# The grouped convolution of a four-layer network on one core: from three-row stacks on four column tiles to 32x32 products on sixteen tiles

## The chip, the cores and the metric

The kernel runs on one core of one Trainium2 chip. The time is the device time of one execution in microseconds (us), as a median over runs. The engines have short names throughout: PE is TensorE's matmul, PEld its weight load, DVE is VectorE, ACT is ScalarE, POOL is GpSimd, SP is SyncE, which here only issues DMAs.

## The reference

The input is a batch of 8 images of 128 channels and 56x56 pixels, all float32. Four layers follow one another, each a residual over a group norm of 32 groups of 4 channels:

```python
def _L2_conv_ref(x, w3, w1, b, p):
    O, I = (w3.shape[0], w3.shape[1])
    i = jnp.arange(O)[:, None]
    j = jnp.arange(I)[None, :]
    m3 = (j - i) % p == 0
    w3m = w3 * m3[:, :, None, None].astype(w3.dtype)
    out = jax.lax.conv_general_dilated(x, w3m, window_strides=(1, 1), padding=((1, 1), (1, 1)), dimension_numbers=('NCHW', 'OIHW', 'NCHW'))
    w1m = w1 * (~m3).astype(w1.dtype)
    out = out + jnp.einsum('oi,bihw->bohw', w1m, x)
    out = out + b.sum(axis=1)[None, :, None, None]
    return out
...
    x = x + _L0_conv_ref(_gn(x), ...)
    x = x + _L1_conv_ref(_gn(x), ...)
    x = x + _L2_conv_ref(_gn(x), L2_conv_w3, L2_conv_w1, L2_conv_b, 4)
    x = x + _L3_conv_ref(_gn(x), ...)
```

Layer 0 is window attention with a depthwise 3x3 convolution. Layer 1 is a recurrence over the 3136 pixels of an image, with 512 hidden values, h = tanh(g + W h). Layer 2, whose code is shown, is a 3x3 convolution in which an output channel sees only the input channels of its own class (index modulo 4), and a 1x1 convolution in which it sees only the channels of the other three classes. Layer 3 is two full 3x3 convolutions with batch norms and a residual.

## The kernel before

The residual stream `X` stays in SBUF, 128 channels on 128 partitions, 8 images of 3136 pixels in the free dimension. The channels are sorted by class, so each class is one quarter of 32 partitions (`CL` = 32). An image has seven blocks of eight rows (`NBLK` = 7, `WS` = 8, 448 pixels), which is one PSUM bank of float32.

**Layer 1** works on 17 pieces of every image at once (`NCH`), two time steps per turn of its loop: per step `step` (L1078) multiplies the gates on PE, DVE adds the input's share (L1098) and ACT takes the tanh (L1100). In the first 186 steps the input's share is computed in the same turn (`shrunk`, L1015: tanh on ACT at L1026, then the subtraction on DVE at L1027; `products`, `gathered`); in the last 56 it is read back from DRAM (`recall`). As pixels become final, `stats` (L983) takes batch norm statistics (`bn_stats`) of the final stretch of image 0, so that layer 2 finds them ready: 8 instructions in all.

**Layer 2** is in `convolutions`. Each image is normalised into a padded copy `pads[b % 2]` of 58x58. `spread` (L1304) makes `g3` from it: for each class three copies of its 32 channels, shifted by 0, 1 and 2 columns, stacked on 96 partitions, so that one product covers the three taps of a row. Of the 12 copies of a chunk of rows, 3 lie on the right partitions and are made by ACT (L1315); 9 cross partitions and are DMAs, issued from the queues of SP and POOL (L1317). An image is spread in three chunks (the first image in five). Per block, `within` (L1321) runs 12 products 96x32: three rows of taps by four classes, each class on its own 32 columns of the array and its own 32 partitions of the bank. `between` (L1332) adds the masked 1x1 as one 128x128 product for two blocks in turn. `add` (L1339) adds bank and bias to `X` on DVE. The class `Norm` (L1254) computes the group norm of one image: seven `bn_stats` and an aggregate on DVE (L1265), a product with `gavg` for the mean and one for the variance over the groups, a root on ACT, a reciprocal, and the normalisation on DVE (`normal`, L1293). The norm of image b + 2 is taken while image b is multiplied. `stats3` (L1403) takes the same statistics of finished blocks of `X` for layer 3's norm.

The order on PE, ACT, DVE and POOL is the program order of the loop over the 56 blocks (a manual schedule); SP's DMAs follow their data. PSUM has four banks for blocks (`ps_c`) and two for norms (`ps_g`). A `warm` call issues idle products to keep the PE's clock up while the first norm is computed. w3, w1 and the mask m1 are loaded by the first three DMAs of the layer, issued by SP (L1235, L1237, L1239).

**Layer 3** transforms columns of the normalised image on DVE and POOL (`column_sums`), multiplies on PE (L1573), and combines on DVE. The norms of its images 1 to 7 are computed together (`Rest`), during the first image; their last statistics, those of image 7, are taken by `stats3` in the first two blocks of layer 3 and one just ahead of it.

A second call of `convolutions` after a slow form of layer 1 stands in a branch that this input does not take.

## Time and profile before

| what | us |
|---|---|
| time, median of 3 runs | 3289.23 (3288.72 to 3290.22) |
| the profiled execution, its own time | 3289.69 |
| its span | 3287.8 |
| stretch 0 to 1190 (layer 0): busy PE / DVE / ACT / POOL | 1141.36 / 960.34 / 656.08 / 914.71 |
| 1190 to 2370 (layer 1, fresh inputs) | 1179.16 / 696.42 / 226.54 / 343.02 |
| 2370 to 2640 (layer 1, inputs read back) | 269.86 / 80.02 / 54.57 / 0.36 |
| 2640 to 2848 (layer 2) | 199.25 / 140.82 / 101.14 / 126.03 |
| 2848 to 3288 (layer 3) | 399.18 / 428.38 / 232.72 / 102.32 |

The rows below the span are busy times of four engines in stretches of the span, in us. They are read stage by stage: an engine whose busy time comes near the length of the stretch sets its pace. The chain that ended last, as the page gives it by engine and by its first lines:

```profile
PE 78%; DVE 15%; issue 2%; POOL 2%; ACT 1%; DMA 1%; ACTq 0%; POOLq 0%; SPq 0%; DVEq 0%
PE ps L1086 27%; PE q L1051 9%; PE s L539 6%; PE po L605 6%; PE po L1116 5%; PE t L581 4%; PE plep L420 4%; PE pc L1327 4%; PE pi L1021 3%; DVE nmax L546 2%; PE t L571 2%; PE py L446 1%; PE pc L1335 1%; PE pvp L319 1%; PE pvt L301 1%
```

L1327 and L1335 are the two kinds of products of layer 2, L1086 is layer 1's recurrence.

### The profile page before, as it was taken

To read this page: it belongs to the slowest core of one execution; us is meant where nothing else is said; L and a number is where in the kernel's file an instruction comes from. 1 tells how busy PE (TensorE), PEld (TensorE's weight loads), DVE (VectorE), ACT (ScalarE), POOL (GpSimd) and SP (SyncE) were. 2 spreads that over 40 slices of the span, in tenths; PEclk is the share of its full clock that TensorE was granted. 3 is DMA by queue.
4 is the path that set the end of the run, shared out by engine and by line. 5 is a ranking of instruction groups with operands and counts; after the bars stand their busy time and mean duration, and the time that the engine had idled before them with its cause. 6 is when DMAs were issued, how large, how long until landed. Compare 5 with 4: busy or idle time off the path is not lost.

```text
span 3287.8 us, 104432 instructions
## 1 busy us (share of the span) xinstructions
PE 3188.8 (97%) x40780; PEld 2690.5 (82%) x40780; DVE 2306.0 (70%) x5747; ACT 1271.0 (39%) x2423; POOL 1486.4 (45%) x4147
## 2 busy tenths in 40 slices
PE   7999999999999989999999999999999999899998
PEld 5767677676776679999999999999999943498998
DVE  5888888788887866665555555555523257799999
ACT  4555555555555522222111111111122244455654
POOL 5787887878787833332222222222100066322221
PEclk8999999999999999999999999999999999999999
DMA  5455555555455411110000000000022156300001
GB/s 155 133 142 133 142 138 134 143 131 142 121 139 148 117 55 49 49 49 22 1 1 1 1 1 1 1 1 1 23 61 61 50 154 165 81 25 35 30 30 41
DMA packets 188167, 239.09 MB, mean 73 GB/s; under 512 B 42848, under 2 KB 137568, under 8 KB 187664
## 3 DMA queue, kind: packets, MB, share of 16 engines
q0 software_dynamic: 40896, 123.47, 13.8%
q1 hardware_dynamic: 130256, 101.95, 10.7%
q10 hardware_dynamic: 16512, 6.90, 0.9%
q8 instruction: 324, 5.31, 0.7%
q14 instruction: 179, 1.47, 0.1%
HBM read 133.64 MB, written 67.56 MB: 61 GB/s over the span
## 4 chain that ended last, share of the span: by engine, by line
PE 78%; DVE 15%; issue 2%; POOL 2%; ACT 1%; DMA 1%; ACTq 0%; POOLq 0%; SPq 0%; DVEq 0%
PE ps L1086 27%; PE q L1051 9%; PE s L539 6%; PE po L605 6%; PE po L1116 5%; PE t L581 4%; PE plep L420 4%; PE pc L1327 4%; PE pi L1021 3%; DVE nmax L546 2%; PE t L571 2%; PE py L446 1%; PE pc L1335 1%; PE pvp L319 1%; PE pvt L301 1%
## 5 line engine op out<-in xcount | busy, mean ns | idle before, releaser
L1086 PE MATMUL ps<-hs,w_gates 128*128 128x136 f32 x7680 | 928.8, 279 | 0.0
L1086 PEld LDWEIGHTS ps<-hs,w_gates 128*128 128x128 f32 x7680 | 911.6, 190 | 4.5
L1100 ACT ACTIVATE hs<-v 128x272 f32<-128x272 f32 x538 | 212.4, 405 | 1167.2 <-DVE v L1098 1167.2
L546 DVE TENSOR_REDUCE nmax<-s 128x2 f32<-128x512 f32 x784 | 486.6, 685 | 166.9 <-PE s L539 165.1
L1098 DVE TENSOR_TENSOR v<-ps,g 128x272 f32<-128x272 f32 x538 | 216.5, 411 | 493.8 <-PE ps L1086 406.6
L591 ACT ACTIVATE e<-t 128x512 f32<-128x512 f32 x784 | 429.7, 596 | 341.2 <-PE t L581 263.1
L1039 POOL TENSOR_TENSOR d<-inp 128x136 f32<-128x136 f32 x186 | 87.8, 472 | 788.9 <-DVE inp L1027 788.9
L498 POOL COPY ks<-kT 128x64 f32 x1568 | 297.2, 235 | 122.8 <-PE t L581 65.5
L605 PE MATMUL po<-e,ring 128*32 128x64 f32 x12544 | 244.9, 230 | 6.9 <-DVE nmax L546 5.7
L605 PEld LDWEIGHTS po<-e,ring 128*32 128x32 f32 x12544 | 217.9, 149 | 31.9 <-DVE nmax L546 8.4
L581 PE MATMUL t<-qm,ks 32*128 32x128 f32 x6272 | 237.8, 273 | 1.5 <-issue 1.5
L539 PE MATMUL s<-ks,qm 32*128 32x256 f32 x3136 | 234.0, 403 | 4.3 <-ACT vp L342 2.1
L581 PEld LDWEIGHTS t<-qm,ks 32*128 32x128 f32 x6272 | 220.6, 187 | 3.6 <-issue 2.3
L1573 PE MATMUL pc3b<-vb,u_w2c_t 128*128 128x196 f32 x1152 | 203.9, 340 | 19.7 <-DVE vb L1554 19.7
L1573 PEld LDWEIGHTS pc3b<-vb,u_w2c_t 128*128 128x128 f32 x1152 | 200.3, 197 | 22.0 <-DVE vb L1554 21.8
L1573 PE MATMUL pc3a<-va,u_w1c_t 128*128 128x196 f32 x1152 | 197.2, 331 | 7.4 <-DVE d_pc3a L1590 3.3
L1116 PE MATMUL po<-hs,xw 128*128 128x272 f32 x744 | 204.0, 397 | 0.2
L1573 PEld LDWEIGHTS pc3a<-va,u_w1c_t 128*128 128x128 f32 x1152 | 192.8, 191 | 10.9 <-issue 8.7
L539 PEld LDWEIGHTS s<-ks,qm 32*128 32x128 f32 x3136 | 146.5, 185 | 34.5 <-DVE logit L364 4.0
L1051 PE MATMUL q<-d,mixed 128*128 128x136 f32 x1116 | 160.2, 279 | 0.5 <-DVE g L1065 0.3
L500 POOL TENSOR_TENSOR qm<-q,hmask 128x128 f32<-128x128 f32 x392 | 154.0, 393 | 0.0
L1116 PEld LDWEIGHTS po<-hs,xw 128*128 128x128 f32 x744 | 132.0, 190 | 22.2 <-ACT hs L1100 0.6
(304 smaller groups left out, 5417.0 us busy)
## 6 DMA issues: line engine op xcount, KB each, us to landing
ring<-vpix SPq DMA_DIRECT2D x1176, 32.0 KB
v<-vimg POOLq DMA_DIRECT2D x56, 290.0 KB, 3.9
v<-vimg POOLq DMA_DIRECT2D x56, 289.5 KB, 4.7
v<-vimg POOLq DMA_DIRECT2D x56, 289.0 KB, 5.6
kept<-g SPq DMA_DIRECT2D x56, 272.0 KB, 2.4
g<-kept SPq DMA_DIRECT2D x56, 272.0 KB, 2.6
xkeep<-X POOLq DMA_DIRECT2D x56, 224.0 KB, 2.6
vimg<-vrow POOLq DMA_DIRECT2D x54, 232.0 KB, 2.5
```

The lines of the kernel that those rows point to most:

```text
L498: nc.gpsimd.tensor_copy(kw[:, t : t + 1, :], ks[b][:, bass.ds(at, 1), :])
L539: nc.tensor.matmul(s_["s"][g][:, o, :], w["qm"][h].rearrange("p h x -> p (h x)"), w["kw"][h], start=True, stop=True,)
L546: nc.vector.tensor_reduce(s_["nmax"][:, :, g], s_["s"][g], AX.X, ALU.max, negate=True)
L581: nc.tensor.matmul(s_["t"][g][:, o, c], w["kw"][h, c * P : (c + 1) * P], w["qm"][h].rearrange("p h x -> p (h x)"), start=False, stop=(o == ...
L591: nc.scalar.activation(s_["e"][g], s_["t"][g], AF.Exp)
L605: mm = nc.tensor.matmul(po[g * CL : (g + 1) * CL, h, o], flat[:, at : at + 8 * CL - 7 : 8], s_["e"][g][:, o, c, h * WPX : (h + 1) * WPX], ...
L1051: nc.tensor.matmul(q[n // 3][:, n % 3], w, x, start=True, stop=True)
L1086: nc.tensor.matmul(ps[f][:, i], whh[:, k, m * P : (m + 1) * P], prev[k // 2][:, (s - 1) % 2, k % 2].rearrange("p c b -> p (c b)"), start=( ...
L1098: nc.vector.tensor_tensor(v[:, i : i + n], ps[f][:, i : i + n], x, ALU.add)
L1100: nc.scalar.activation(to, x, AF.Tanh)
L1116: nc.tensor.matmul(po, wout[:, k, :], hs[k // 2][:, :, k % 2], start=(k == 0), stop=(k == KH - 1))
L1573: nc.tensor.matmul(bank[:, half].rearrange("p (y x) -> p y x", x=H4), u[:, dy, k, :], v[:, k, i * RB + dy : i * RB + dy + RB, :], start=(d ...
```

## The change

**Layer 2's products.** The three-row stacks and `g3` go. Every product is now 32x32: input class k on the 32 rows of row group k, output class on 32 columns. The four row groups share the work of a block: each carries its own quarter of the 1x1 (for its own class this quarter holds the centre tap of the 3x3, which has been put into the 1x1's weights with the mask) and two of the eight outer taps of all four classes. For a tap, row group k needs class c on its own partitions: from `pads` where c is k, otherwise from one of three shifted copies `turned[0..2]`, which hold the image with its quarters turned by one, two or three. A block takes 3 x 16 products, in what follows three slots of 16. Row group k works on a block five slots (`LAG`) later than row group k - 1, so the four row groups work at four different blocks, and `ps_c` has seven banks, `ps_g` one. The order between two row groups that write the same bank is made by a token: after a slot in which a row group finished a block, POOL writes one element (`memset`), which waits for PE; the first product of the next row group on that bank waits for that token.

**Its inputs.** `plain` normalises a chunk of rows into `pads` (on DVE for image 0, on ACT afterwards), `swapped` normalises two halves on ACT into `turned[1]` with the upper and lower 64 partitions exchanged, and `shifted2` fills `turned[0]` and `turned[2]` by DMAs of 32 partitions out of `pads`, one on SP's queue and one on POOL's (for the first two chunks of image 0 and row group 0, DVE writes them directly). The first image has five chunks, later ones four.

**Norms.** The statistics of all eight images are taken in layer 1, six parts for each, where before this was done for image 0 only; at most one in a turn of the loop of two steps, two in a turn near the end. The last two parts of each image follow in layer 2. The norms are computed for image 0, for image 1 and for images 2 to 7 together. Layer 3's norm of image 0 has a norm of its own (`few3`), and `stats3` runs for all blocks up to the 53rd within layer 2; four remain for layer 3, and the one ahead of it is dropped.

**Weights.** `w3_c` now holds eight taps in the order of the row groups; `w3_m`, the centre taps, is a new input of 128x128. SP loads w1, m1, wm and then w3.

```diff
         def stats(b, j):
...
+            nc.vector.bn_stats(st2[:, b, j, :], part)
...
-                    stats(len(cuts) - 2 - len(done))
-                    if len(done) == 1:
-                        stats(len(cuts) - 2)
+                    spans = [len(cuts) - 2 - len(done)] + [SPANS - 3] * (len(done) == 1)
+                    known_.extend((b, j) for b in range(B) for j in spans)
                     done.pop(0)
+                for b, j in known_[: 1 if len(done) else 2]:
+                    stats(b, j)
+                del known_[: 1 if len(done) else 2]
...
-            ps_g = l2.enter_context(tc.tile_pool(name="ps_g", bufs=2, space=PSUM))
+            ps_g = l2.enter_context(tc.tile_pool(name="ps_g", bufs=1, space=PSUM))
...
-            ps_c = p2.enter_context(tc.tile_pool(name="ps_c", bufs=4, space=PSUM))
+            ps_c = p2.enter_context(tc.tile_pool(name="ps_c", bufs=7, space=PSUM))
+            turned = [padded(pool2, f"turned{j}", [P, PW, PW]) for j in range(3)]
...
-            g3 = pool2.tile([3 * CL, 4, PW * PW], F32, name="g3")
...
+            w1, m1, wm = (pool2.tile([P, P], F32, name=n) for n in ("w1", "m1", "wm"))
+            for t, n in ((w1, "w1_t"), (m1, "m1"), (wm, "w3_m")):
+                nc.sync.dma_start(t, a[n])
+            w3 = pool2.tile([P, 2, 4, CL], F32, name="w3")
             nc.sync.dma_start(w3, a["w3_c"])
...
+            def plain(b, rows, scalar=True):
+                lo, hi, x = inside(b, rows)
+                dst = pads[b % 2][:, lo:hi, 1 : 1 + HW]
+                if scalar:
+                    nc.scalar.activation(dst, x, AF.Identity, bias=of2[:, b : b + 1], scale=rs2[:, b : b + 1])
+                else:
+                    nc.vector.tensor_scalar(dst, x, gm2[:, b : b + 1], rs2[:, b : b + 1], ALU.subtract, ALU.mult)
+
+            def swapped(b, rows, h):
+                lo, hi, x = inside(b, rows)
+                to, of = slice(64 * h, 64 * h + 64), slice(64 - 64 * h, 128 - 64 * h)
+                nc.scalar.activation(
+                    turned[1][to, lo:hi, 1 : 1 + HW], x[of], AF.Identity,
+                    bias=of2[of, b : b + 1], scale=rs2[of, b : b + 1],
+                )
+
+            def shifted2(b, rows, k, direct=False):
+                lo, hi, x = inside(b, rows)
+                for j in (0, 2):
+                    c = (k + 1 + j) % 4
+                    to, of = slice(k * CL, (k + 1) * CL), slice(c * CL, (c + 1) * CL)
+                    if direct:
...
+                    else:
+                        (nc.sync, nc.gpsimd)[j // 2].dma_start(
+                            turned[j][to, rows[0] : rows[1], :], pads[b % 2][of, rows[0] : rows[1], :]
+                        )
...
+            RING = [(y, x) for y in range(3) for x in range(3) if (y, x) != (1, 1)]
+            ROWS, LAG, passed = 4, 5, {}
+            mark = few.tile([1, 1], F32, name="mark", bufs=1)
+            DONE = [(LAG * k + 2) // 3 for k in range(ROWS)]
...
+            def taps(t):
+                for s in range(3 * t, 3 * t + 3):
+                    left = False
+                    for k in range(ROWS):
+                        n, part = divmod(s - LAG * k, 3)
+                        if not 0 <= n < B * NBLK:
+                            continue
+                        b, i = divmod(n, NBLK)
+                        if part == k == 0:
+                            pcs[n] = ps_c.tile([P, WS, HW], F32, name=f"pc2_{n}", tag="pc")
+                        own = slice(k * CL, (k + 1) * CL)
+                        for c in range(4):
+                            if part == 0:
+                                w, src, y, x = w1[own, c * CL : (c + 1) * CL], pads[b % 2], 1, 1
+                            else:
+                                w, (y, x) = w3[own, part - 1, c, :], RING[2 * k + part - 1]
+                                src = pads[b % 2] if c == k else turned[(c - k - 1) % 4]
+                            mm = nc.tensor.matmul(
+                                pcs[n][c * CL : (c + 1) * CL], w,
+                                src[own, i * WS + y : (i + 1) * WS + y, x : x + HW],
+                                start=(k == 0 and part == 0), stop=(k == ROWS - 1 and part == 2),
+                                skip_group_check=True,
+                            )
+                            if k and part == c == 0:
+                                after(mm.ins, passed[s - (LAG - 2)])
+                        left = left or (part == 2 and k < ROWS - 1)
+                    if left:
+                        token = nc.gpsimd.memset(mark, 0.0)
+                        after(token.ins, mm.ins)
+                        passed[s] = token.ins
...
+            first, second, others = Norms(0, 1), Norms(1, 2), Norms(2, B)
+            few3 = Groups(mv3[:, 0:1, :], few.tile([P, 1], F32, name="gm3", bufs=1), "l3_0")
+            LAST = B * NBLK - 4
...
                 nc.vector.tensor_mul(w1, w1, m1)
+                nc.vector.tensor_mul(m1, wm, m1)
+                nc.vector.tensor_sub(wm, wm, m1)
+                nc.vector.tensor_add(w1, w1, wm)
+                first.root()
+                first.invert()
+                for n, rows in enumerate(BEGIN):
+                    plain(0, rows, False)
+                    swapped(0, rows, 0)
+                    if n < 2:
+                        shifted2(0, rows, 0, True)
+                    swapped(0, rows, 1)
...
+                starts = (0, 1, 2, 4, 6)
+                for _, n, k in sorted((3 * starts[n] + LAG * k, n, k) for n in range(5) for k in range(4)):
+                    if n > 1 or k:
+                        shifted2(0, BEGIN[n], k)
+                second.stats(1)
+                for t in range(B * NBLK + DONE[-1]):
+                    b, i = divmod(t, NBLK)
+                    taps(t)
...
+                    if t < 6:
+                        others.stats(2 + t)
...
+                    n = t - DONE[-1]
+                    if n >= 0:
                         add(n)
+                    if 0 < n <= LAST:
+                        stats3(*divmod(n - 1, NBLK))
+                    for to in (b, b + 1):
+                        if not 1 <= to < B:
+                            continue
+                        at = t - NBLK * (to - 1)
+                        if 2 <= at <= 5:
+                            plain(to, CHUNKS[at - 2])
+                        for rows, i0, free in zip(CHUNKS, (0, 2, 4, 6), (2, 4, 6, 6)):
+                            for h in range(2):
+                                if at == free + DONE[2 * h + 1]:
+                                    swapped(to, rows, h)
+                            if at - free in DONE:
+                                shifted2(to, rows, DONE.index(at - free))
```

The loop's turn t issues the three slots 3t to 3t + 2; with `LAG` = 5 the last row group finishes block t - 5 in turn t (`DONE[-1]` = 5). Lines of the changed kernel that the prediction names: the products and their weight loads L1381, the token's memset L1391, the DMAs of `shifted2` L1346, the statistics of layer 1 L988.

## The prediction

> **What bounds the kernel now.** I read the stages first, then the instructions of layer 2 by line, then the timeline of one steady stretch and of the start of the layer. The first view gives, for a stretch, busy time (and count) of PE, PEld, DVE, ACT, POOL, then the granted TensorE clock, the DMA share and GB/s.
>
> ```profile
> 2700.00:2720.00 20.00, 20.00 (x168) 6.94 (x164) 14.08 (x35) 6.58 (x12) 9.30 (x19) 1.00 0.51 134
> ...
> 3000.00:3120.00 120.00, 113.34 (x651) 112.14 (x650) 119.20 (x266) 71.20 (x84) 31.61 (x38) 0.96 0.09 33
> ```
>
> Layer 2 (first row) is TensorE's: it is never idle, VectorE is 70% busy. Layer 3 (second row) is VectorE's: 119.2 of 120 us. So matmul time counts in layer 2 and VectorE time in layer 3.
>
> ```profile
> L1327 PE MATMUL pc<-g,w x1344: 537/538/954, 2654.4 to 2843.2; 96*32 96x448 f32 x192
> ...
> L1335 PE MATMUL pc<-pad,w x112: 538/539/643, 2661.6 to 2844.9; 128*128 128x448 f32 x112
> ```
>
> 672 and 56 products leave 1344 and 112 records: one f32 product is two passes.
>
> ```profile
> 2670.12 4.72 PE L1327 MATMUL pc<-g,w 96*32 96x448 f32 x48
> 2670.52 0.13 PEld L1327 LDWEIGHTS pc<-g,w 96*32 96x32 f32 x4 [0.25 <-issue]
> ...
> 2670.90 0.13 PEld L1327 LDWEIGHTS pc<-g,w 96*32 96x32 f32 x4 [0.25 <-issue]
> ...
> 2676.47 4.72 PE L1327 MATMUL pc<-g,w 96*32 96x448 f32 x48
> ```
>
> Four weights are loaded every 0.38 us (2670.52, 2670.90): four column tiles run one pass together, in the time that one full-array pass takes. I call 0.75 us, two passes of 448 columns, a slot. A block is 3 slots of taps and one of the 1x1; two blocks take 6.35 us (2670.12 to 2676.47), which is 8 x 0.75 and 0.35 for the two changes of tile shape.
>
> ```profile
> 2646.32 0.34 SPq L1235 DMA_DIRECT2D w<-in_w_c_dram  x1
> ...
> 2647.70 11.79 POOL L1317 DMA_DIRECT2D g<-pad  x23 [0.73 <-DVE pad L1298]
> ...
> 2654.41 7.04 PE L1327 MATMUL pc<-g,w 96*32 96x448 f32 x48 [2.42 <-DMA g<-pad]
> ...
> 2848.00 18.30 PE L1573 MATMUL pc3a<-va,u_w1c_t 128*128 128x196 f32 x108 [2.56 <-DVE va L1554]
> ```
>
> Products run from 2654.41 to 2845.45 (the last L1335 group starts at 2843.67 and lasts 1.78); layer 3's first comes 2.55 us later. POOL issues a DMA every 0.51 us.
>
> **The sum, step by step.** Times are on the profile's clock, whose run took 3289.69 us (span 3287.8), 0.46 above the median.
>
> *Steady work.* 48 products of 32x32 per block on 16 tiles are 3 slots instead of 4, with no change of tile shape. The last row group trails the first by 15 slots, so there are 56 x 3 + 15 = 183 slots. No row shows 16 tiles at work, only four, in one column (L1327) or one row group (L581) each. The bounds of a slot are 0.75 (the streaming time; nothing here streams 448 columns faster, so there is no gain below it) and 3.0 (four products at a time, as the rows show). I take 0.75, because whichever of the two ways the four tiles lie they cost each other nothing, and because issue is no limit: the group of 64 records of L605 at 702.89 lasts 1.24 us, at most 19.4 ns for a matmul with its load, and 32 such are 0.62 us.
>
> A rule against it: the Trainium skill ("TensorE: Matmul & The Clock Gate", section "Measured speedup vs the span model") has sixteen tiles gain 10.6 times, not 16, and three column tiles 2.38. By that a slot would be an estimated 0.75 x 16/10.6 = 1.13 us and the kernel about 3313 us; but the second figure does not hold in this stream, where four column tiles take the 0.375 us of one.
>
> *Start.* The masked centre tap puts four 128x128 VectorE operations (0.28 us, L1470) ahead of the reciprocal, and they need wm. It is the third DMA, where m's is now (SP's row at 2647.18), and w's, the first, took 2.3 us from issue to landing: 2649.5. Three operations (0.84) and two small ones (0.3) give the first normalisation at 2650.7, not 2646.61. The first slot needs one chunk (0.8, the 504 form of L1298) and starts at 2651.4; slots 0 to 4 have one row group alone. Slot 5 waits for the first POOL memset, and in POOL's order 18 DMA issues stand ahead of it. The second of them waits for the third chunk: 3 x 0.80 + 3 x 0.50 + 0.74 = 4.6 us after 2650.7, the four direct copies on VectorE included. 17 more at 0.50 us are 8.5, and some half microsecond goes to landings, since POOL has eight in flight at a time and they take 2 to 5 us: 13.7 us, slot 5 at 2664.4. Slots 5 to 182 are 178 x 0.75 = 133.5: 2797.9.
>
> *Waits on POOL.* Every slot from the sixth on waits for a memset on POOL that itself waits for the slot three before. With POOL free there is room: a slot's products end 0.17 us after the next begins (538 ns against 375), and 0.1 for the semaphore, 0.15 for the memset (a 128x14 one takes 0.11) leave over 1 us. But what is queued on POOL ahead of it are L1346's DMAs. In three iterations of each image it is late, counted from the end of the iteration, where 2.25 us are free: two iterations put four DMAs there (0.42 to the memset, 4 x 0.5, then 0.15 + 0.1: 2.67, late 0.42). In a third, a DMA waits for a normalisation on ACT behind a swapped copy (0.27, two ACT operations of 0.97 by the 32x928 copy of L1315, one DMA, the same ends: 3.04, late 0.79). 7 + 6 times 0.42 and 6 times 0.79 make 10.2 us. With the memset between 0.1 and 0.3 this is 8.7 to 15.
>
> *Small products.* Five of them (statistics of images 2 to 7, layer 3's first image, the verdict) fall into the stream. In the trace two blocks with one between take 2.70 for 2.25 (2682.83 to 2685.53): 5 x 0.45 = 2.3.
>
> *Clock.* Layer 2's restart in the trace, after 2.4 us idle, was granted 0.93 of the clock over the stretch 2654 to 2680: 1.8 us lost. Slot 5 comes after 9 us: between 1.7 and 3.4, I take 3.4.
>
> Sum: 2797.9 + 10.2 + 2.3 + 3.4 + 0.2 (tail) = 2814.0 for the end of the products, 31.4 us before 2845.45.
>
> *What costs nothing.* The 42 extra statistics of layer 1 take 0.68 us each on VectorE, one behind each second step. There VectorE waits 0.87 us for ACT (line at 2326.41), so it fits by 0.2; in the recall half two find 3.4 us.
>
> ```profile
> 2325.09 0.44 DVE L1098 TENSOR_TENSOR v<-ps,g 128x272 f32<-128x272 f32 x1 [0.48 <-PE ps L1086]
> ...
> 2326.41 0.91 DVE L1027 SCALAR_TENSOR_TENSOR inp<-pi,bine,th 128x272 f32<-128x272 f32 x2 [0.87 <-ACT th L1026]
> ...
> 2386.60 0.68 DVE L984 BATCH_NORM_STATS2 st<-X 128x6 f32<-128x512 f32 x1
> ```
>
> Without that cover they are 42 x 0.68 = 28.6 us on the chain of steps. ACT takes 4 normalisations and 8 half copies an image, about 10.3 us of 17; its lateness is in the 0.79. Add and next statistics, 0.68 + 0.61, fit VectorE's 2.25 us, and seven banks leave the add 1.3 us of room. SP issues 16 DMAs an image at 0.54, 8.7 us. A DMA has some 7 us to land.
>
> *Layer 3* loses four of VectorE's statistics and one aggregate, 0.6 us each and 0.35: 2.8 us on the engine that bounds it.
>
> 31.4 + 2.8 = 34.2: 3289.69 - 34.2 = 3255.5, at the median's level **3255 us**. Its own range is 3247 to 3270: slots of 0.75 to 0.80, the memset's bounds, the clock's.
>
> **Rivals.** (a) *The array does not hold sixteen streams.* Matmuls that share a column or row group take turns, so the slot is longer. For: no row shows more than four tiles. At eight together the slot is 1.5 us, the waits on POOL vanish in it, and the products end 281 us after 2650.7, 86 us late: about 3375. At four together 183 x 3.0 gives some 3640. The turning point is a slot of about 1.0 us: 192 + 2.3 + 3.4 after 2650.7 is 2848. Against: the 0.375 us of the rows in both directions. 0.16, slower.
> (b) *POOL's queue is worse than counted*, or a slot is 0.9: landing times hold up POOL, the memset is late in more iterations. A further 3 us an image is 20 us: 3275. For: in the group of L1317's DMA issues POOL's queue waited 9.7 us for landings. 0.12, still faster.
> (c) *VectorE in layer 1 has no room*: statistics delay the next shrink by their 0.68. 28.6 us given back: 3284. Against: the three such instructions already there stand in the same gap. 0.03.
> (d) *TensorE stops being the bound* and POOL and ACT set the old pace, or a slot of 1.0: 3289. 0.05.
>
> **How the numbers follow.** The forecast has 0.64, and time is that of its own sum. Within 0.2% (6.6 us, about what a measurement of this kernel can tell from no change) counts as same. Faster: 0.64 + 0.12 + 0.02 = 0.78; same 0.06; slower 0.16. The range 3246 to 3290 takes in (b), (c) and most of (d); (a), the rest of (d) and a little on the other side, some 0.2, are left out.
>
> **What would show it.** Loads of L1381 in sets of 16 every 0.375 us, a block per 2.25 us: the slot. A gap of 8 to 10 us before the sixth slot ended by a POOL memset: the start. Three short waits on POOL per image of 0.4 to 0.8 us. L988 with nothing behind it that is later than before. The first product of layer 3 near 2816. Sets of four or eight, or a stage of over 195 us, prove me wrong.

## The result, and the profile after

The changed kernel takes 3298.06 us (median of 16 runs, 3293.12 to 3302.73), the kernel before 3288.89 us over 16 runs. The ratio is 1.0029, with a 95% interval of 1.0021 to 1.0036: 9.2 us slower. The forecast was 3255, its range 3246 to 3290.

The profiled execution of the changed kernel has a span of 3295.2 us. I cut both spans at three events that the two kernels share (layer 3's first product counts from its weight load, 0.03 us ahead of it):

| stretch, us | before | after | difference |
|---|---|---|---|
| start to the first tanh of layer 1 (layer 0) | 1196.19 | 1203.02 | +6.83 |
| to its last tanh (layer 1) | 1443.93 | 1444.23 | +0.30 |
| to layer 3's first product (layer 2) | 207.85 | 209.60 | +1.75 |
| to the end (layer 3) | 439.79 | 438.34 | -1.45 |

So the layer that was rewritten gained nothing in this pair, and most of the loss stands in a layer that the change doesn't touch. Layer 2 has some spread of its own. In three profiles of this same layer 2 it took 209.60, 211.86 and 215.30 us, in three of the one before 207.85, 205.68 and 208.78: 212.3 against 207.4 on average. By these means about half of the 9.2 us is layer 2's own.

The timeline of the changed kernel from the last tanh to layer 3 (start, duration, engine, line, tile, count, and in brackets the idle time before it with what ended it):

```profile
2647.25 0.43 ACT L1104 ACTIVATE hs<-v 128x272 f32<-128x272 f32 x1 [0.56 <-DVE v L1102]
...
2659.39 1.31 PE L1381 MATMUL pc<-pad,w 32*32 32x448 f32 x9
...
2664.69 0.59 PE L1266 MATMUL pm_l<-mv_l,c_gavg 128*128 128x1 f32 x2 [2.85 <-DVE mv_l L1300]
...
2671.35 0.50 POOL L1346 DMA_DIRECT2D turned<-pad  x1 [0.24 <-issue]
2671.84 0.09 POOL L1391 MEMSET mark<- 1x1 f32 x1
2671.98 0.20 PEld L1381 LDWEIGHTS pc<-pad,w 32*32 32x32 f32 x8 [3.59 <-POOL mark L1391]
...
2856.88 20.08 PE L1652 MATMUL pc3a<-va,u_w1c_t 128*128 128x196 f32 x108 [3.01 <-DVE va L1633]
```

The sixth slot starts at 2671.98, 12.6 us behind the first product, when POOL comes to the token behind its DMA issues. From there to the last product's end at 2853.87 it is 181.9 us.

The stretches of layer 2 and layer 3 (busy time and count of PE, PEld, DVE, ACT, POOL, then granted clock, DMA share, GB/s):

```profile
2665.00:2670.00 5.00, 4.91 (x26) 1.16 (x25) 1.60 (x7) 1.86 (x3) 4.71 (x10) 0.50 1.00 250
2670.00:2675.00 5.00, 3.02 (x26) 1.03 (x34) 0.43 (x3) 0.33 (x2) 1.30 (x5) 0.50 1.04 249
2675.00:2680.00 5.00, 5.00 (x65) 1.66 (x58) 4.47 (x15) 3.16 (x3) 0.55 (x3) 0.50 0.41 125
2700.00:2720.00 20.00, 19.29 (x636) 12.07 (x612) 10.84 (x29) 10.66 (x13) 8.86 (x35) 1.00 0.69 162
...
3009.00:3129.00 120.00, 112.21 (x659) 110.43 (x658) 119.42 (x265) 70.00 (x84) 32.99 (x39) 0.99 0.09 34
```

Two things are to be seen. The granted clock is at a half until past 2680. And in 2700 to 2720, at full clock, there are 636 matmul records, 32 to a slot: 19.9 slots in 20 us, a slot of 1.0 us where the forecast had 0.75. VectorE fell from 70% to 54% of that stretch, and still bounds layer 3.

All 5376 passes are on record, one f32 product being two passes:

```profile
L1381 PE MATMUL pc<-pad,w x2688: 531/535/949, 2659.4 to 2853.3; 32*32 32x448 f32 x192
L1381 PE MATMUL pc<-turned,w x2688: 531/533/949, 2660.2 to 2853.3; 32*32 32x448 f32 x192
```

By its record, whose end the profile models, a single pass takes no longer than before (535 ns median, 538 before), and passes of many tiles overlap: 32 of them start in a slot of 1.0 us. Only the slot is longer than 0.75. POOL's queue shows the rhythm, since it writes one token a slot:

```profile
2801.09 1.98 POOL L1346 DMA_DIRECT2D turned<-pad  x4 [0.39 <-issue]
2803.06 0.23 POOL L1391 MEMSET mark<- 1x1 f32 x2
...
2804.26 0.49 POOL L1346 DMA_DIRECT2D turned<-pad  x1 [0.39 <-issue]
2804.74 0.09 POOL L1391 MEMSET mark<- 1x1 f32 x1
2805.68 0.09 POOL L1391 MEMSET mark<- 1x1 f32 x1 [0.85 <-PE pc L1381]
2806.64 0.09 POOL L1391 MEMSET mark<- 1x1 f32 x1 [0.86 <-PE pc L1381]
...
2845.72 0.09 POOL L1391 MEMSET mark<- 1x1 f32 x1 [1.42 <-PE pc L1381]
2846.47 0.09 POOL L1391 MEMSET mark<- 1x1 f32 x1 [0.66 <-PE pc L1381]
```

At 2805.68 and 2806.64 POOL waits for PE, and the tokens are 0.96 apart: that is the slot of sixteen products, with nothing ahead of it. (The token at 2804.74 comes right behind a DMA issue, so its distance to the next tells less.) The median over 132 slots is 0.951, the mean 1.025; where POOL waited for PE at both tokens, which it did at 33 pairs, the median is 0.95 too. At 2845.72 the first row group has run out of blocks, a slot has twelve products, and it takes 0.75. At 2801.09 four DMA issues hold two tokens, which then come together.

### The profile page after: what moved, and what is told of

Same layout as the page of the kernel before. It is cut to its first block, busy times and chain, and to the rows that moved or that the text cites. A ratio compares the mean times of both kernels' runs of the same rounds, so it can differ in the third digit from the quotient of the medians.

```text
span 3295.2 us, 112081 instructions
## 1 busy us (share of the span) xinstructions
PE 3187.4 (97%) x44680; PEld 2741.2 (83%) x44680; DVE 2283.7 (69%) x5718; ACT 1273.4 (39%) x2392; POOL 1447.5 (44%) x4211
## 4 chain that ended last, share of the span: by engine, by line
PE 78%; DVE 14%; issue 3%; POOL 2%; ACT 1%; DMA 1%; ACTq 1%; POOLq 0%; SPq 0%; DVEq 0%
PE ps L1090 27%; PE q L1055 9%; PE po L605 5%; PE po L1120 5%; PE s L539 5%; PE pc L1381 5%; PE t L581 4%; PE plep L420 4%; PE pi L1025 3%; DVE nmax L546 2%; PE t L571 2%; PE py L446 1%; PE pc3b L1652 1%; PE pvp L319 1%; PE pvt L301 1%
## 5 line engine op out<-in xcount | busy, mean ns | idle before, releaser
L1104 ACT ACTIVATE hs<-v 128x272 f32<-128x272 f32 x538 | 212.3, 404 | 1167.6 <-DVE v L1102 1167.6
L1381 PE MATMUL pc<-pad,w 32*32 32x448 f32 x2688 | 182.7, 555 | 3.6 <-POOL mark L1391 3.5
L1381 PE MATMUL pc<-turned,w 32*32 32x448 f32 x2688 | 177.9, 553 | 3.1 <-issue 3.1
```

The costliest lines, as they stand in the source:

```text
L1381: mm = nc.tensor.matmul(pcs[n][c * CL : (c + 1) * CL], w, src[own, i * WS + y : (i + 1) * WS + y, x : x + HW], start=(k == 0 and part == 0 ...
```

## The experiments

Ratios are against runs of the kernel before on the same chip. "Layer 2" is the time from the last tanh to layer 3's first product in the profiled execution.

### What makes a slot 0.95 us

**One wide product for the 1x1's quarter.** Its four products have the same input, so one of 32x128 does the same with 10, 13 and 13 products in a slot:

```diff
+                        if part == 0:
+                            mm = nc.tensor.matmul(
+                                pcs[n], w1[own], pads[b % 2][own, i * WS + 1 : (i + 1) * WS + 1, 1 : 1 + HW],
+                                start=(k == 0), stop=False, skip_group_check=True,
+                            )
...
-                        for c in range(4):
+                        for c in range(4) if part else ():
```

> The quarter of the 1x1 that a row group carries is one 32x128 product instead of four 32x32 ones with the same input: a slot has 10, 13 and 13 products in turn instead of 16. In the changed kernel a slot with all four row groups lasts 0.95 us, and in its last 15 slots, with 12 and 8 products, 0.755 and 0.753. Theory 1 (the products are handed out at 29.7 ns a pass with its load): slots of 0.75 to 0.77, 178 slots x 0.19 = 33 us less, of which some 8 come back as waits for POOL: about 3273. Theory 2 (four streams that write the same 32 columns of the array share something, 0.475 us a pass instead of 0.375): no change, 3298. Theory 3 (0.2 us a slot for the waits on the tokens): no change, 3298. Theory 4 (a change of tile shape costs 0.17 us, as between L1327 and L1335 before): two changes a slot, about 3350.

3887.47 us, ratio 1.1823 (1.1803 to 1.1842). Theory 4 had the change of shape, but not what else comes with it. PE in that kernel:

```profile
2750.57 1.86 PE L1376 MATMUL pc<-pad,w 32*128 32x448 f32 x2
2752.35 0.96 PE L1388 MATMUL pc<-turned,w 32*32 32x448 f32 x2
...
2753.15 0.95 PE L1388 MATMUL pc<-pad,w 32*32 32x448 f32 x1
2754.03 1.11 PE L1376 MATMUL pc<-pad,w 32*128 32x448 f32 x1
```

The wide product runs alone, then the small ones, then a wide one. Products of the two shapes take turns (their records overlap by under 0.1 us, two passes of one shape by 0.2), and the clock is at 0.50 from 2659.1 us to the end of the layer. A turn lasts 1.78 or 1.68 us in these rows: two passes of 0.75 us at that clock, and some 0.2 for the change. A slot is three turns, 5.13 us by the median. So the price of a change was about right; that the shapes would not overlap, and at half the clock, was not in theory 4. The Trainium skill ("TensorEngine Tiling (Array Packing)", section "Key Properties") says that a change of tiling mode drains the engine; these rows agree. The run tells nothing of theories 1 to 3.

**Half the stream, and three quarters of the products.** These two kernels, and the three after them except the one with another order, leave out or mix up part of layer 2, so only their slots are compared, not their times.

```diff
-                                src[own, i * WS + y : (i + 1) * WS + y, x : x + HW],
+                                src[own, i * WS + y : i * WS + WS // 2 + y, x : x + HW],
...
```

> Every product streams four of the eight rows of its block, 224 columns instead of 448; the other half of the pixels is left out of layer 2. Theory 1 (handing out): the slot of 16 products stays at 0.95 us. Theory 2 (four streams share a column): half of 0.95, 0.475, or 0.53 where handing out at the 16.7 ns between two starts takes over. Theory 3 (0.2 us for the tokens): 0.375 + 0.2 = 0.575.

```diff
-                        for c in range(4):
+                        for c in range(3):
...
```

> The products of the fourth output class are left out: 12 products a slot, four row groups on three columns of tiles, all tokens kept. Theory 1 (handing out): 24 x 29.7 ns = 0.71, so the streams set 0.75. Theory 2 (four streams in a column): 0.95. Theory 3 (tokens): 0.95.

The tokens where POOL waits for PE, with half the stream and then with three classes:

```profile
2722.81 0.09 POOL L1391 MEMSET mark<- 1x1 f32 x1 [0.50 <-PE pc L1381]
2723.38 0.09 POOL L1391 MEMSET mark<- 1x1 f32 x1 [0.49 <-PE pc L1381]
2723.96 0.09 POOL L1391 MEMSET mark<- 1x1 f32 x1 [0.49 <-PE pc L1381]
```

```profile
2798.45 0.09 POOL L1391 MEMSET mark<- 1x1 f32 x1 [0.66 <-PE pc L1381]
2799.21 0.09 POOL L1391 MEMSET mark<- 1x1 f32 x1 [0.66 <-PE pc L1381]
2800.01 0.09 POOL L1391 MEMSET mark<- 1x1 f32 x1 [0.71 <-PE pc L1381]
```

With half the stream, such slots mostly last 0.58 to 0.63: not 0.95, so it isn't the 29.7 ns a pass at which theory 1 hands them out, and not half of 0.95. With three classes they last 0.75 to 0.80, with all tokens and with four row groups to a column: so neither the tokens nor four streams in a column cost the 0.2. Theories 1 to 3 fell, each by one of the two runs. What fits both is a limit on passes in flight (theory 5, in the next expectation).

**Fourteen products, another order, and eight tall products.**

```diff
-                        for c in range(4):
+                        for c in range(4 if k < 2 else 3):
...
```

> Row groups 2 and 3 leave out the products of the fourth output class: 14 products a slot instead of 16, all tokens kept. Theory 5 (formed after the runs with 224 columns and with three classes: at most 16 passes are in flight, and each is in flight for its stream and 0.1 us more; 32 x 0.475 / 16 = 0.95, 32 x 0.2875 / 16 = 0.575, 24 x 0.475 / 16 = 0.71): 28 x 0.475 / 16 = 0.83 us a slot. Rival (the array loses time only when every tile is taken): 0.75 to 0.80. Rival (0.2 us for each slot): 0.95.

```diff
-                    for k in range(ROWS):
...
+                    for c in range(4):
+                        for k in range(ROWS):
...
```

> Within a slot the products go by output class first and row group second, instead of row group first; the same 16 products. Theory 5 (at most 16 passes in flight): the order is of no account, the best stretch of 4 us hands out as many passes as in the changed kernel (145, 0.88 us a slot) and the median distance of two tokens stays at 0.95. Rival (four products of one row group next to each other wait for one another, a matter of order): 0.75 to 0.85, or clearly more than 0.95.

```diff
-            ROWS, LAG, passed = 4, 5, {}
+            ROWS, LAG, passed = 2, 5, {}
...
-                        own = slice(k * CL, (k + 1) * CL)
+                        own = slice(k * 2 * CL, (k + 1) * 2 * CL)
```

> Two row groups of 64 rows instead of four of 32: a slot has 8 products of 64x32 that take up the whole array, with the same streams, LAG and copies. What is multiplied is not the convolution (two of the four row groups' taps are left out and classes are mixed); it is a look at the slot alone. Theory 5 (at most 16 passes in flight): 8 products leave room, 0.75 us a slot. Rival (the array loses time when all its rows and columns are taken, which 12 and 14 products of 16 did not or did less): 0.95.

To compare them I took all product starts between 2692 and 2805 us and measured how long three slots' worth of them takes, per slot; the limits of the fastest twentieth and the fastest quarter of these stretches are least disturbed by waits. Theory 5 stands with the streaming time where that is longer:

| products a slot | stream | fastest twentieth | fastest quarter | theory 5 |
|---|---|---|---|---|
| 16 of 32x32 | 448 | 0.89 | 0.94 | 0.95 |
| 16, other order | 448 | 0.90 | 0.95 | 0.95 |
| 14 of 32x32 | 448 | 0.79 | 0.83 | 0.83 |
| 12 of 32x32 | 448 | 0.75 | 0.76 | 0.75 |
| 8 of 64x32 | 448 | 0.75 | 0.75 | 0.75 |
| 16 of 32x32 | 224 | 0.59 | (0.83, waits) | 0.575 |

Eight products that take up the whole array run at the streaming time, and sixteen do not, in either order. So it is not that the array is full, nor the order. "At most sixteen passes in flight, each for its stream and 0.1 us" comes near all six rows, but it isn't shown. The run with fourteen was to decide between it (0.83) and its rival that time is lost only when all sixteen tiles are taken (0.75 to 0.80), and it doesn't. Its stretches lie between, and by the tokens where POOL waits for PE twice running, fourteen take what twelve do, 0.80 by the median (27 and 26 pairs):

```profile
2731.44 0.09 POOL L1391 MEMSET mark<- 1x1 f32 x1 [0.85 <-PE pc L1381]
2732.19 0.09 POOL L1391 MEMSET mark<- 1x1 f32 x1 [0.67 <-PE pc L1381]
2733.00 0.09 POOL L1391 MEMSET mark<- 1x1 f32 x1 [0.71 <-PE pc L1381]
```

A third reading was not tested: a limit on the output written at a time. Eight tall products write half of what sixteen write. The half stream would then take 0.475, or by the 17 ns that lie between two starts 32 x 0.017 = 0.54, where the fastest stretch of three slots took 0.54 and the fastest twentieth 0.59. What sets the 0.95 therefore stays open; that it is 0.95 with sixteen small products at once, and 0.75 with twelve, is measured.

### Where the tokens should be

**All copies' DMAs on SP**, so that POOL has only tokens:

```diff
-                        (nc.sync, nc.gpsimd)[j // 2].dma_start(
+                        nc.sync.dma_start(
```

> All DMAs of the shifted copies are issued by SP, none by POOL, so that nothing stands ahead of the tokens on POOL. If the tokens' lateness is what makes a steady slot last 1.13 us on average instead of 0.95, and POOL's 18 issues are what held the sixth slot until 2672: the sixth slot 8 us earlier, some 3.4 us an image less, and less of the half clock, about 3266. Rival: SP cannot issue 32 DMAs an image in 21 us (it took 15.13 us for the first 18), the copies come late, PE waits for them: 3290 to 3310.

3311.43 us, ratio 1.0065 (1.0048 to 1.0082). The rival held: the sixth slot came earlier (its token 2.5 us behind the first product instead of 12.5), and then PE waited 9.9 us for copies; the mean slot (between the 25th and the 157th token, here and below) rose to 1.164.

**The tokens on VectorE.**

```diff
-                        token = nc.gpsimd.memset(mark, 0.0)
+                        token = nc.vector.memset(mark, 0.0)
```

> The token is a memset on VectorE instead of POOL; the DMAs stay where they are. Theory (POOL's DMA issues stand ahead of the tokens): the mean slot between the 25th and the 157th token, 1.025 us now, falls to 0.95 to 0.97, and the sixth slot, held to 2671.98 by POOL, starts 5 to 7 us earlier, right behind VectorE's work on the first image; together 13 to 19 us: about 3282. Rival (VectorE's own work stands ahead of the tokens, or the copies come late): mean slot of 1.0 or more, 3290 to 3300.

3296.47 us, ratio 1.0024 (1.0014 to 1.0034). The start improved by 7 us, the mean slot rose to 1.099. The rival held again. Tokens now stand behind VectorE's own work; how much of the loss that makes, against copies that come late, isn't shown.

**One DMA a slot on POOL.**

```diff
+                        if j and spare is not None:
+                            spare.append(copy)
...
+                    if spare:
+                        spare.pop(0)()
...
+                for f in (spare or ())[:3]:
+                    f()
```

> The DMAs that POOL issues are spread: of the first image's 18, three stand ahead of the loop, and all others go one behind each slot's token instead of in batches of up to four between two iterations. Theory (batches of DMA issues delay the tokens): the mean slot between the 25th and 157th token falls from 1.025 to 0.96, and the sixth slot starts 6 to 9 us earlier than the 12.6 us behind the first product; together 13 to 18 us less in layer 2, about 3283. Rival (the slots wait for something else, copies that come later now): mean slot over 1.0, 3293 to 3300.

3291.07 us, ratio 1.0008 (0.9998 to 1.0018), layer 2 206.3 us. POOL's queue:

```profile
2804.27 0.50 POOL L1347 DMA_DIRECT2D turned<-pad  x1 [0.40 <-issue]
2804.75 0.09 POOL L1398 MEMSET mark<- 1x1 f32 x1
2805.28 0.49 POOL L1347 DMA_DIRECT2D turned<-pad  x1 [0.43 <-issue]
2805.76 0.09 POOL L1398 MEMSET mark<- 1x1 f32 x1
```

Tokens come within their slots now: of 132 distances 27 were under 0.3 us, pairs that had been held together, and one is left. The median distance is 0.966. But the mean stayed at 1.024 where I expected 0.96, so the held tokens were not what the mean slot lost: the row groups catch up. The sixth slot's token came 5.1 us behind the first product instead of 12.5, which alone is as much as the gain of some 7 us in the time, half of what I expected. A few long waits remain. The longest, 3.9 us from token to token, is still POOL's order, a DMA that waits for PE with two tokens behind it:

```profile
2723.86 0.50 POOL L1347 DMA_DIRECT2D turned<-pad  x1 [3.33 <-PE pc L1388]
2724.35 0.23 POOL L1398 MEMSET mark<- 1x1 f32 x2
```

### Layer 0, which the change does not touch

**The kernel before again, and with a longer tile.** The one thing that the change does ahead of layer 0 is to make `st2` larger (192 to 1536 bytes a partition), which moves everything placed behind it.

> The kernel before, unchanged, for one more look at layers 0 and 1: the last tanh of layer 1 came at 2640.1 us of the span before, and at 2647.3, 2642.2, 2644.3, 2643.4 and 2648.5 in the changed kernel and its four variants. Theory A (layer 0 varies between executions by some us, whatever the kernel): the last tanh anywhere between 2638 and 2648. Theory B (the change moves something that layer 0 feels, such as addresses): 2639 to 2641.

```diff
-    st2 = const.tile([P, 8, 6], F32, name="st2")
+    st2 = const.tile([P, 128], F32, name="st2")[:, :48].rearrange("p (j s) -> p j s", s=6)
```

> The kernel before with its statistics tile st2 made longer, from 192 to 512 bytes a partition, so that what is placed behind it stands at the same offset modulo 512 bytes as in the changed kernel; nothing else. If addresses modulo 512 slow down layer 0: last tanh at 2643 to 2648, about 3293. If not: 2640, 3289.

The kernel before had its last tanh at 2638.97 (2640.12 in the first profile). With the longer tile alone it is 2644.88, and the time is 3294.89, ratio 1.0014 (1.0005 to 1.0024), 5.9 us more by the medians. The packets of POOL's DMA queue in the first 1190 us took 187.0 ns on average over all their records, not 180.5 and 180.1. The page's lines of this queue (packets, MB, share of sixteen DMA engines' span), for the kernel before and for it with the longer tile:

```profile
q0 software_dynamic: 40896, 123.47, 13.8%
```

```profile
q0 software_dynamic: 40896, 123.47, 14.2%
```

The same packets and bytes take 3% more of the engines. All profiles on record fall in two groups: in the fourteen with packets of 185.9 to 187.6 ns the first tanh came at 1198.0 to 1204.3, 1200.9 on average, in the four with 180.1 to 181.5 ns at 1195.1 to 1197.0, 1196.0 on average. So it costs about 5 us, and the 6.8 of the first pair is partly chance.

**The changed kernel with other lengths of `st2`.** First 64 bytes more, then folded to 1216 bytes, which is 192 modulo 512 as before the change:

> The changed kernel with its statistics tile 64 bytes a partition longer (1600 instead of 1536), so that what is placed behind it stands at the same offset modulo 128 bytes as before the change (192 bytes then). The kernel before with that tile at 512 bytes was 5.9 us slower, all of it in layer 0, where POOL's DMA packets took 187.0 ns instead of 180.5. If 128 bytes are what counts: first tanh of layer 1 at 1195 to 1197 us of the span instead of 1198 to 1204, packets at 180, about 3292. If not (other addresses, or another cause): 1198 to 1204, 187 ns, 3298.

```diff
-    st2 = const.tile([P, B, 8, 6], F32, name="st2")
+    st2 = const.tile([P, 304], F32, name="st2")
+    stat = lambda b, lo, hi: st2[:, (B - 1 - b) * 36 + lo * 6 : (B - 1 - b) * 36 + hi * 6]
```

> The changed kernel with its statistics tile folded to 1216 bytes a partition (the two last parts of an image lie on the first two of the image before it, which are used up by then), so that everything behind it stands at the offset modulo 512 bytes that it had before the change (192). If that offset is what made layer 0 slower: POOL's packets at 180 to 181 ns instead of 187, the first tanh of layer 1 at 1195 to 1197 us instead of 1198 to 1204, about 3292 in all. If not: 187 ns, 1198 to 1204, 3298.

1600 bytes: packets 185.9 ns, first tanh at 1200.47, 3296.19 us. 128 bytes was not the rule. 1216 bytes: 180.6 ns, first tanh at 1196.99, as before the change. The time was 3294.86, ratio 1.0016 (1.0007 to 1.0025): layer 0 is repaired, layer 2 keeps its loss (215.3 us in this profile). So the length of `st2`, that is where the tiles behind it lie, is the cause of layer 0's loss. Which of the tiles behind it matters, and why 192 modulo 512 is good where 0 and 64 are not, stays open; 1664 bytes (128 modulo 512), which the run with idle products in the gap has below, were no better (first tanh at 1202.06).

### The half clock

**Idle products in the gap.** The spread DMAs, and 14 products of `warm` ahead of the sixth slot:

> The spread DMAs of the run before, and 14 idle 128x128 products ahead of the sixth slot, where PE sat idle for 3.4 us and the granted clock then was 0.5 for 17 us (2659.8 to 2677.3 there). If the idle gap is what takes the clock: it stays at 1.0 or drops for 3 to 4 us as before the change, 6 to 9 us less than the run with spread DMAs in layer 2 (206.3 us from the last tanh to layer 3's first product, so 198 to 200). Rival (slots of 8 and 12 small products don't count as work enough for the clock): 0.5 all the same, 204 to 207. The statistics tile is 1664 bytes a partition long here; that acts on layer 0 alone (first tanh of layer 1 at 1195 to 1197 if the offset is a good one, 1198 to 1204 if not). Time about 3282, or 3277 with the good offset.

3291.31 us, ratio 1.0002 (0.9993 to 1.0011), layer 2 207.45. The clock was at 0.5 from 2664 to 2672 all the same, and the 14 products themselves ran in it: the gap stands ahead of L1266, so they came too late, and the run doesn't tell whether filling the gap helps.

**The norm of image 1 a turn later**, in the kernel with spread DMAs, which takes L1266's wait out of the way:

```diff
-                    if t == 0:
+                    if t == 1:
                         second.mean_mm()
...
```

> The run with spread DMAs, and the norm of image 1 one turn later: its two small products stand behind the slots of the second and third turn instead of the first and second. In the runs so far PE stood 2.9 us at the first of them, waiting for VectorE's aggregate of image 1, with slots that could run behind it; the granted clock fell to 0.5 in that gap and stayed there for 17 us. The fill of the run before stood behind that product and so came too late. Expected: PE runs slots 3 to 5 at once, the clock stays at 1.0 or drops for under 5 us, and from the last tanh to layer 3's first product it takes 195 to 200 us instead of 206.3; about 3281. Rival (the slots with 4 and 8 small products, or a wait for the copies, bring the clock down all the same): 203 to 207, 3288 to 3291.

3291.16 us, ratio 1.0006 (0.9997 to 1.0015), layer 2 206.5. The rival held:

```profile
2658.00:2662.00 4.00, 4.00 (x48) 1.35 (x40) 3.87 (x9) 3.92 (x5) 1.18 (x3) 1.00 0.40 100
2662.00:2674.00 12.00, 11.61 (x119) 4.01 (x127) 6.64 (x25) 6.34 (x8) 5.10 (x15) 0.50 0.82 208
```

PE is busy 15.6 of 16 us, and the clock falls to a half behind four microseconds of slots with four products. Idle time is not needed for it.

**All tiles busy from the first slot.** The run before, the folded `st2`, and idle 32x32 products on row groups that have no block yet:

```diff
+                        if n < 0 and idle:
+                            for c in range(4):
+                                nc.tensor.matmul(
+                                    idle[k - 1][c * CL : (c + 1) * CL],
+                                    w1[k * CL : (k + 1) * CL, c * CL : (c + 1) * CL],
+                                    pads[0][k * CL : (k + 1) * CL, 1 : 1 + WS, 1 : 1 + HW],
+                                    start=True, stop=True, skip_group_check=True,
+                                )
```

> The run with spread DMAs and the later norm, the folded statistics tile, and idle 32x32 products on the row groups that have no block yet in slots 0 to 14 (into three spare banks), so that all 16 tiles are busy from the first slot. If the clock falls because the slots at the start fill a quarter or half of the array: it stays at 1.0 (or falls for under 5 us), from the last tanh to layer 3's first product 196 to 200 us instead of 206.5, and about 3278 in all. Rival (the clock falls for another reason, such as the waits on tokens and copies at the start): 0.5 for 10 us or more, 205 to 208, about 3286.

3283.18 us, ratio 0.9984 (0.9975 to 0.9993): 6.3 us faster than the kernel before, and the best of all. The clock:

```profile
2658.00:2660.00 2.00, 2.00 (x67) 1.10 (x65) 1.66 (x9) 1.64 (x3) 1.82 (x5) 1.00 0.97 231
2660.00:2662.00 2.00, 2.00 (x65) 1.03 (x36) 0.46 (x3) 0.00 (x0) 0.66 (x3) 1.00 1.00 289
2662.00:2664.00 2.00, 2.00 (x72) 1.13 (x74) 1.49 (x6) 1.46 (x3) 0.98 (x2) 1.00 0.85 208
```

It stays at 1.00 throughout the layer's start, so the sparse slots took it. Layer 2 fell only to 205.4 us, not below 200. PE now stands still later (2.1 us between 2672 and 2676, and the 3.9 us wait of the run with spread DMAs is there too), by what I did not try to settle. And at the layer's end, where the row groups run out of blocks and the slots are sparse again, the clock fell 4.5 us before the last product's end (at a half that is an estimated 2 us), while in the run before it held until the products were done:

```profile
2838.00:2842.00 4.00, 4.00 (x25) 1.68 (x17) 0.68 (x1) 0.00 (x0) 0.00 (x0) 0.50 0.00 0
```

Of the 8 us against the run before it, 5.5 are layer 0's (first tanh at 1195.80 instead of 1201.26).

## Why the prediction was wrong, point by point

**The slot: this step failed.** I took 0.75 "because whichever of the two ways the four tiles lie they cost each other nothing, and because issue is no limit". Both halves were read from rows with four products at a time, and neither says what sixteen do. A slot of sixteen takes 0.95, 153 slots have all four row groups, and 153 x 0.2 = 31 us, which is the gain expected of layer 2 almost to the microsecond. What the runs showed in its place: 0.95 us for sixteen products at a time, 0.75 for twelve, by a limit that stays open. My bounds of 0.75 and 3.0 held the truth; between ends that far apart I picked the lower end itself. My turning point fits too: at a slot of 1.0 I had priced the kernel at 3289 (rival d) and gave that 0.05; with its waits the slot came to 1.025, and layer 2 took 1.75 us more than before in the first pair, 4.9 on average.

The rule that I set aside was a little nearer than my reading. The Trainium skill ("TensorE: Matmul & The Clock Gate", section "Measured speedup vs the span model") lets sixteen tiles gain 10.6 times, not 16. The slot that I estimated from it, 1.13, was 0.18 too long, where 0.75 was 0.20 too short. Here the gain is 16 x 0.75/0.95 = 12.6, and the measurement decides; but I refuted the rule with four tiles, where it also fails here, and took that for a refutation at sixteen.

**The start: right.** Sixth slot predicted 13.0 us behind the first product, measured 12.6, and the cause is the one named: the token behind POOL's DMA issues.

**Waits on POOL and small products: the sum fits, the mechanism doesn't.** 12.5 us predicted for 178 slots; over the 132 slots counted, (1.025 - 0.951) x 132 = 9.8 against 9.3. But 10.2 of the 12.5 were tokens held behind batches of POOL's DMAs, three short waits an image. Between 2690 and 2850 the trace has five waits of PE's weight loads that a token ended, 3.5 us together, and the run with spread DMAs took the held pairs away without any change of the mean slot. So the agreement is in good part luck, and most of the 9.8 us has no cause shown. My sums were off besides: the terms named for the third iteration make 2.96 us, not 3.04, and a memset of 0.1 to 0.3 us gives 9.3 to 13.1 by these terms, not 8.7 to 15.

**The clock: right in kind, too small.** 3.4 us predicted; at a half from the sixth slot on to some 2683, 11 us, it took 5.6. I thought of an idle gap. There is one here (2.85 us ahead of L1266), but the runs without it and with filled tiles put the fall down to the sparse slots.

Together, with the 9.8 us carried over to 153 slots as 11: 133.5 + 31 + 11 + 5.6 = 181 us from the sixth slot to the end, where the trace has 181.9.

**Layer 1: right.** 42 more statistics cost 0.3 us. The row behind one of them, where VectorE waited 0.87 us for ACT before:

```profile
2265.24 0.68 DVE L988 BATCH_NORM_STATS2 st<-X 128x6 f32<-128x512 f32 x1
2266.20 0.91 DVE L1031 SCALAR_TENSOR_TENSOR inp<-pi,bine,th 128x272 f32<-128x272 f32 x2 [0.27 <-ACT th L1030]
```

Of the gap 0.27 us are left.

**Layer 3:** 1.45 us less, where 2.8 were predicted; two more profiles of the same layer 3 have 438.22 and 440.01 us, so the size is within its spread.

**Layer 0: missed.** I read the larger `st2` as a matter of space. That it moves what lies behind it, and that this costs about 5 us in another layer, was in none of my terms, and no row of the trace before could have told its size.

## What to carry to other kernels

Time won by putting more small products side by side has to be read from a row with as many of them at once; where none exists, keep the middle of the bounds and not the end. Fewer and taller products (64x32) filled the array at the streaming time where sixteen small ones did not. A change of a tile's size moves every tile behind it: compare the untouched layers first, before you explain the one you changed.

## What the runs showed of the hardware

- Sixteen 32x32 products at a time: 0.95 us for two passes of 448 columns; fourteen 0.79 to 0.83, twelve, and eight of 64x32, 0.75; sixteen with 224 columns 0.59.
- Products of 32x128 and 32x32 in one stream took turns: 5.13 us for a slot of three turns, at half the clock.
- The granted clock fell to 0.5 while PE was busy 97% of the time, with four to eight products of 32x32 at once, and stayed at 1.00 when idle products filled the other tiles.
- With the same packets and bytes, the DMA packets of POOL's queue took 187.0 ns or 180.5 ns in layer 0, with nothing changed but the length of one tile and so the place of those behind it.
